# A two-layer graph network on one Trainium2 core: two destination blocks of attention 1 moved from dense steps to gathers

## The chip, the cores and the metric

The kernel runs on one core of a Trainium2 chip. The metric is device time in microseconds, the median of several executions. One further execution was recorded by the hardware profiler; all shares, durations and waits below come from that one.

## The reference

The input is a graph of 6250 nodes with 128 features and 200,000 edges, sorted by destination. Two residual blocks follow one another:

```python
h = relu(layernorm(x))
x = x + gat_2(elu(gat_1(h)))          # two attention layers
h = relu(layernorm(x))
x = x + conv(h, src, dst, edge_attr_4, edge_attr_8)

def gat_layer(x, W, attn_l, attn_r):   # H heads of D features
    feat = x @ W
    el, er = sum(feat * attn_l), sum(feat * attn_r)       # per node and head
    e = leaky_relu(el[src] + er[dst], 0.2)
    alpha = softmax of e over the edges of each dst
    return segment_sum(feat[src] * alpha, dst)
```

The first attention layer (attention 1) has four heads of 16 features, the second has one head. The convolution makes a message for each edge from the source's features and the edge's attributes and sums it by destination.

## The kernel before, in words

Nodes lie in NB = 49 blocks of P = 128. Attention 1 works on one destination block at a time, and in two different ways.

**Gathered blocks** are the first NG = NB - DENSE1 blocks, so 31. A window of 128 x 34 edges (K = 34) covers the edges of a block. `attending` takes them in five groups (`GROUPS`: four of 8 columns, one of 2). For each column `gather` (L319) has POOL issue one indirect DMA that fetches 128 rows of `table1` into the tile `G`, of which there are six buffers. `attend` then builds a one-hot of the destinations (`ohr`, L328, DVE), multiplies the transposed one-hot `oht` by the destination factors (L364, PE), forms weights and messages (L366 to L371, DVE), splits the messages into two halves (L335 on ACT, L336 on DVE) and sums them by destination on PE (L381). `load_low` fetches the 1088 KB from which `oht` is made, once for each block. After each fourth block, and after the last gathered one, `finish1` turns the sums into the tables of attention 2.

**Dense blocks** are the other DENSE1 = 18, taken in nine pairs by the generator `dense1`. They need no gathers: for every (source, destination) pair of nodes the number of edges is known, in `counts`. For each group of HS = 7 source blocks and each of the four heads, one step makes 7 ramps (L889, ACT), takes their minimum with the counts into `up` (L891, DVE), and later multiplies `up` by the source's features on PE (L909, 14 matmuls); once for each source group, PE also sums `every` (L903, 14 matmuls). A pair has a beginning (the tile `erb`), 4 x 7 such steps and an end. For each source group SP loads eight pieces of counts (`ctc`) and one of `rhs1` (`rc`, 717.5 KB), one group ahead.

**Counting** makes `counts` for all 49 blocks, in 196 steps of a quarter block: DVE makes one-hots `lo` and `key` (L771), PE multiplies them (L782), ACT copies the result (L784) and stores it. Attention 2 needs the counts of every block; the dense blocks of attention 1 need theirs before they are loaded.

The main loop runs over the gathered blocks and their groups, and hands out the other two kinds of step in proportion to the gathers done. Counting starts with block LAG = 3, dense steps with block LAG_D = 5:

```python
split = NG // (P // WB) * (P // WB)
order = [*range(split, NB), *range(split)]
n_dense = -(-DENSE1 // 2) * (2 + H1 * (NB // HS))
...
due = len(steps) * ((b - LAG) * K + s + n) // ((NG - LAG) * K)
...
due = n_dense * ((b - LAG_D) * K + s + n) // ((NG - LAG_D) * K)
```

`order` is the order of counting, beginning with the dense blocks. `n_dense` is 270. A step's later half (the scatter on PE, the matmuls of `up`) is issued one step later. The order written so is that of the program; the compiler's scheduling may shift single instructions on an engine's queue against it, and each queue then runs in its order.

Behind attention 1 all engines read a flag (L480) that decides whether blocks are done again. Then attention 2 runs, dense in all 49 blocks, and after it the convolution with 1563 gathers of its own.

Of the kernel before, what the change touches and what calls it, by code (L numbers as in the profile page):

```python
# [52 lines left out]
CT, LT = 30, 40  # L53
LAG = 3
AHEAD = 4
DENSE1, LAG_D = 18, 5
GP, GK, GSB = 125, 16, 4
SEG = 40
FAR = 1.0e30
# [1389 lines left out]
```

## Time and profile before

| what | us |
|---|---|
| median of 3 runs | 4578.62 (4572.18 to 4579.08) |
| profiled execution | 4562.61 |
| its span, first to last instruction | 4560.9 |
| first gather of attention 1 | at 110.4 |
| first gather of block 5 | at 389.3 |
| last gather of attention 1 begins | at 1751.7 |
| first work behind the flag at the end of attention 1 | at 1846.6 |

Times "at" are counted from the start of the span. In a line of a group, the columns are: line of the program, engine, operation, output and input tiles, shapes and count; then busy time and the mean of one in ns; then the idle time of the engine just before these instructions and what ended it. A line of a window holds its limits and length, busy time with the count of instructions for each engine, the granted TensorE clock as a share, the mean busy share of the DMA engines and the GB/s moved.

### The profile page before, as it was taken

The numbers are of one execution on the slowest core, as the hardware profiler recorded it, in microseconds if no ns is written. First come the engines' busy times: TensorE is split into PE (matmuls) and PEld (weight loads), VectorE is DVE, ScalarE is ACT, GpSimd is POOL, SyncE is SP. The second block draws the span as 40 slices with busy tenths as digits, with TensorE's granted clock in tenths as the row PEclk, the third lists the DMA queues.
The fourth block names the chain that finished last, engine by engine and source line by source line (L and its number), as shares of the span: only waits on it lengthen the run. The fifth ranks groups of instructions, "written<-read, shape, count | busy, mean of one in ns | idle before, by whom it ended". The sixth has DMA issues, their size and how long they took to land. (4 is left out here: it accounts for less than half of the span.)

```text
span 4560.9 us, 65476 instructions
## 1 busy us (share of the span) xinstructions
PE 3204.0 (70%) x21547; PEld 2371.8 (52%) x21548; DVE 3493.8 (77%) x5690; ACT 2829.5 (62%) x6841; POOL 2779.0 (61%) x2684
## 2 busy tenths in 40 slices
PE   4026576767776666499986777777777777777777
PEld 3015566656666666488884444444444444444444
DVE  5258687878887787588886788878778887877877
ACT  2025678788788788499985555555555555555554
POOL 0767777766766672100004777777777777777774
PEclk9998666666666676699997777677677767766776
DMA  4255555555555553544441222222222222222221
GB/s 109 67 140 147 149 155 159 157 155 158 167 161 149 150 166 120 209 156 152 170 156 44 59 59 59 58 56 59 58 59 58 58 57 57 59 58 58 58 58 32
DMA packets 348026, 480.87 MB, mean 105 GB/s; under 512 B 190601, under 2 KB 236207, under 8 KB 343694
## 3 DMA queue, kind: packets, MB, share of 16 engines
q1 hardware_dynamic: 199590, 240.46, 17.1%
q0 software_dynamic: 85776, 147.31, 12.9%
q10 hardware_dynamic: 62296, 88.68, 5.5%
q8 instruction: 176, 2.88, 0.3%
q14 instruction: 188, 1.54, 0.1%
HBM read 367.21 MB, written 108.97 MB: 104 GB/s over the span
## 5 line engine op out<-in xcount | busy, mean ns | idle before, releaser
L319 POOL DMA_INDIRECT G<-table,srcc x1563 | 1589.6, 1017 | 1028.4 <-DVE kept L1229 552.3
L319 POOL DMA_INDIRECT G<-table,srcw x1054 | 1118.0, 1061 | 510.5 <-issue 277.7
L1281 PE MATMUL whole<-halves,ohr 128*128 128x512 f32 x1563 | 681.2, 593 | 358.4 <-DVE halves L336 319.5
L889 ACT ACTIVATE ramp<-erb,sel 128x256 bf16<-128x256 f32 x1764 | 757.3, 499 | 15.5 <-DVE up L891 12.1
L1281 PEld LDWEIGHTS whole<-halves,ohr 128*128 128x128 f32 x1563 | 424.6, 286 | 602.0 <-DVE halves L336 390.5
L1262 ACT ACTIVATE g<-G,a 128x128 f32<-128x128 f32 x1563 | 510.2, 394 | 37.0 <-DMA G<-table,srcc 28.6
L1180 ACT ACTIVATE ramp<-small,sel 128x256 bf16<-128x256 f32 (+1 forms) x1225 | 447.8, 625 | 63.2 <-DVE up L1184 31.9
L784 ACT CAST ca<-small 128x392 bf16<-128x392 f32 x784 | 343.1, 482 | 189.5 <-PE small L782 179.2
L909 PE MATMUL up<-rc,up 128*128 128x102 bf16 x3528 | 311.2, 264 | 167.5 <-DVE up L891 166.2
L782 PE MATMUL small<-key,lo 128*128 128x98 bf16 x3136 | 316.1, 252 | 81.5 <-ACT ca L784 72.7
L909 PEld LDWEIGHTS <-up 128*128 128x128 bf16 x3528 | 266.5, 129 | 195.6 <-DVE up L891 189.4
L1251 PEld LDWEIGHTS big<-wtp_sb,hid 64*128 64x128 f32 x3126 | 259.1, 241 | 204.1 <-ACT hid L1245 100.0
L381 PE MATMUL whole<-halves,ohr 128*128 128x136 f32 x1054 | 231.9, 372 | 178.4 <-DVE halves L336 127.6
L336 DVE TENSOR_TENSOR halves<-big,halves 128x1024 fp32r<-128x1024 f32 x196 | 237.9, 1214 | 143.5 <-ACT halves L335 143.3
L1243 PE MATMUL small<-hid,wm_sb 128*128 128x512 f32 x392 | 289.4, 829 | 72.1 <-ACT hid L1241 72.1
L891 DVE TENSOR_TENSOR up<-ramp,ctc 128x1792 bf16<-128x1792 bf16 x252 | 273.9, 1088 | 85.7 <-ACT ramp L889 72.6
L1251 PE MATMUL big<-wtp_sb,hid 64*128 64x128 f32 x3126 | 310.0, 346 | 26.8 <-ACT hid L1245 26.8
L771 DVE TENSOR_TENSOR lo<-slots,turned 128x2048 bf16<-128x2048 bf16 x196 | 239.3, 1221 | 104.8 <-PE small L782 100.7
L1241 ACT ACTIVATE hid<-small 128x512 f32<-128x512 f32 x196 | 116.9, 596 | 312.8 <-PE small L1239 312.6
L782 PEld LDWEIGHTS <-lo 128*128 128x128 bf16 x3136 | 247.0, 124 | 112.9 <-issue 100.0
L335 ACT CAST halves<-mid 128x1024 fp32r<-128x1024 f32 x196 | 204.1, 1041 | 161.8 <-DVE mid L1270 160.1
L381 PEld LDWEIGHTS whole<-halves,ohr 128*128 128x128 f32 x1054 | 203.1, 278 | 190.2 <-DVE halves L336 135.6
(292 smaller groups left out, 6209.5 us busy)
## 6 DMA issues: line engine op xcount, KB each, us to landing
counts<-ca ACTq DMA_DIRECT2D x196, 392.0 KB
ct<-counts SPq DMA_DIRECT2D x196, 392.0 KB
rc<-rhs SPq DMA_DIRECT2D x63, 717.5 KB
oht<-dlow SPq DMA_DIRECT2D x31, 1088.0 KB
ctc<-counts SPq DMA_DIRECT2D x504, 56.0 KB
G<-table,srcc POOLq DMA_INDIRECT x1563
G<-table,srcw POOLq DMA_INDIRECT x1054
a8t<-attr_rows SPq DMA_DIRECT2D x391, 16.0 KB
```

What stands on the lines that cost most here:

```text
L319: nc.gpsimd.indirect_dma_start(out=G[:, c, :], out_offset=None, in_=table, in_offset=bass.IndirectOffsetOnAxis(ap=idx[:, c:c + 1], axis=0))
L381: nc.tensor.matmul(acc, oh[:, c, :], ms[:, c].rearrange("e s f -> e (s f)"), start=start and c == 0, stop=stop and c == n - 1)
L782: nc.tensor.matmul(ps[:, k * NKEY:(k + 1) * NKEY], lo[:, a, :, r], ky[:, a, :, r], start=True, stop=True)
L784: nc.scalar.copy(ca[:, :, i * W:(i + WBANK) * W].rearrange("p h (k d) -> p h k d", d=W), ps[:, :WBANK * NKEY].rearrange("p (k h d) -> p h ...
L889: nc.scalar.activation(ramp[:, i, :n * P], erb[:, h, :n * P], AF.Relu, bias=sel1[:, h0 + i, h:h + 1], scale=STEEP)
L891: nc.vector.tensor_tensor(up[:, :, :n * P].rearrange("p h (a d) -> p h a d", d=QN), ramp[:, :, :n * P].rearrange("p h (a d) -> p h a d", d ...
L909: nc.tensor.matmul(ups[k][:, h], up[:, i, k * P:(k + 1) * P], by_head[:, i, :, h, :], start=h0 + i + h == 0, stop=h0 + i + h == NB + H1 - 2)
L1180: nc.scalar.activation(ramp[:, h, :n * P], pe[:, :n * P], AF.Relu, bias=sel2[:, h0 + h, :], scale=STEEP)
L1243: nc.tensor.matmul(ph[:, :npr * P], wm2_sb, hid1[:, :npr * P], start=True, stop=True)
L1251: nc.tensor.matmul(pw[:, c, :], hid2[half, j * P:(j + 1) * P], wtp_sb[half].rearrange("x p u -> x (p u)"), start=True, stop=True)
L1262: nc.scalar.activation(g0[:, c], G[:, c, :], AF.Copy, scale=a0[:, c, :])
L1281: nc.tensor.matmul(acc, oh[:, c, :], ms[:, c].rearrange("e s h i u -> e (s h i u)"), start=start, stop=stop)
```

## The change

The number of dense blocks goes from 18 to 16.

```diff
-DENSE1, LAG_D = 18, 5
+DENSE1, LAG_D = 16, 5
```

All else follows from the constant. NG becomes 33, so blocks 31 and 32 are gathered, with 34 gathers and five groups each, and the pairs of dense blocks are eight, from (33, 34) to (47, 48). `n_dense` becomes 240, spread over blocks 5 to 32 instead of 5 to 30; the 196 counting steps are spread over blocks 3 to 32, and their order begins with block 32 instead of 30. The last group of `finish1` for gathered blocks has one block instead of three.

## The prediction

> **What bounds the kernel now.** I read the page's busy line and slices first, then the groups of lines for the shapes the edit touches, then the windows and the waits of attention 1 alone.
>
> ```profile
> PE 3204.0 (70%) x21547; PEld 2371.8 (52%) x21548; DVE 3493.8 (77%) x5690; ACT 2829.5 (62%) x6841; POOL 2779.0 (61%) x2684
> ...
> DVE  5258687878887787588886788878778887877877
> ACT  2025678788788788499985555555555555555554
> POOL 0767777766766672100004777777777777777774
> ```
>
> One slice is 114 us. POOL's row shows three stages: attention 1 with its gathers up to slice 16, attention 2 without POOL (zeros), and the convolution. Only attention 1 contains what is edited. In the timeline it ends at 1846.6 us, where all engines read a branch flag (L480); what follows is untouched, so the change is worth what it moves that instant.
>
> ```profile
> L319 POOL DMA_INDIRECT G<-table,srcw x1054 | 1118.0, 1061 | 510.5 <-issue 277.7 <-DVE w L366 74.3 <-DVE wseg_i L631 62.2
> L889 ACT ACTIVATE ramp<-erb,sel 128x256 bf16<-128x256 f32 x1764 | 757.3, 499 | 15.5 <-DVE up L891 12.1 <-DMA ctc<-counts 2.0 <-DMA counts<-ca 0.8
> L909 PE MATMUL up<-rc,up 128*128 128x102 bf16 x3528 | 311.2, 264 | 167.5 <-DVE up L891 166.2
> L891 DVE TENSOR_TENSOR up<-ramp,ctc 128x1792 bf16<-128x1792 bf16 x252 | 273.9, 1088 | 85.7 <-ACT ramp L889 72.6 <-DMA ctc<-counts 9.1 <-PE up L909 2.0
> L328 DVE TENSOR_TENSOR ohr<-slots,dstw 128x1024 fp32r<-128x1024 bf16 (+1 forms) x155 | 163.3, 1054 | 0.0
> ```
>
> A gather keeps POOL 1.061 us, and 0.30 us of issue precedes nearly each one, so a gathered block of K = 34 costs POOL some 46.3 us. The windows of the stage's steady part, and one block inside it:
>
> ```profile
> core 0: us, PE busy (x) PEld busy (x) DVE busy (x) ACT busy (x) POOL busy (x), PEclk, DMA share, GB/s
> 664.91:717.47 52.56, 36.41 (x368) 33.39 (x369) 40.94 (x65) 42.58 (x106) 40.27 (x39) 0.69 0.53 162
> ...
> 601.95:1846.57 1244.62, 846.21 (x8284) 771.74 (x8283) 987.78 (x1771) 1004.06 (x2490) 803.07 (x750) 0.66 0.52 153
> ```
>
> ACT is busy 1004.1 / 1244.6 = 81%, DVE 79%, PE 68%; POOL is 65% busy and, with its issue time, near 85%. No engine is full: ACT (ramp), DVE (up) and PE (up) hand each other work in order. Who leads is told by POOL's waits. In two groups of the page's fifth part, taken for 390 to 726 us and for 726 to 1696 us:
>
> ```profile
> L319 POOL DMA_INDIRECT G<-table,srcw x238 | 254.5, 1069 | 73.3 <-issue 65.8 <-DMA G<-table,srcw 4.6 <-DVE msg L371 1.0
> L319 POOL DMA_INDIRECT G<-table,srcw x613 | 656.0, 1070 | 284.8 <-issue 157.6 <-DVE w L366 74.0 <-DVE msg L371 16.6
> ```
>
> First POOL waits for nothing: blocks 5 to 11 start every (726.25 - 389.26) / 7 = **48.1 us**, its own pace with the run fetches between. From 726 us it waits until DVE frees a G buffer, and blocks start every (1695.07 - 726.25) / 18 = 53.8 us. So attention 1 is bound by the **ACT-DVE-PE chain**, with POOL 10% behind it as the next bound.
>
> **What the Trainium skill says.** "ScalarE: Activation LUTs", section "What ACT_TABLE_LOAD costs", gives an ACTIVATE with a pointer bias 280 ns + 0.833 ns per element, neighbours overlapping by 93 ns: 493 ns for 256 elements. The trace agrees: median 493 ns, 671.4 us busy for 1563 in the steady window, 0.43 us each. "GPSIMD Engine Reference", section "Key points", names POOL as the only engine for indirect gathers, so the added ones can go nowhere else; all 1054 are on POOL here. "Perfetto Trace Analysis", section "DMA Instruction — SWDGE (GPSIMD)", says the recorded interval is descriptor generation, not the move, so 1.061 us is queue time. "SBUF — State Buffer", section "SBUF: two separate sides", says some DVE modes lock POOL out of writing descriptors; gathers here range from 0.939 to 3.185 us beside a busy DVE, which fits but does not single that out.
>
> **The change part by part.** Two blocks leave the dense steps: 9 pairs become 8. The blocks with dense work become 28 (5 to 32) instead of 26, so a block carries 240/28 = 8.6 dense steps for 270/26 = 10.4, and 196/30 = 6.5 counting steps for 7.
>
> Removed, one pair, 28 steps (4 heads by 7 groups of seven source blocks):
> - ACT: 196 ramps x 0.43 = 84 us, with two erb copies and a copy of every, -86.
> - DVE: 28 x 1.088 = 30.5, and the end's reductions and products about 3.5: -34.
> - PE: 392 of 3528 up matmuls, 311.2/9 = 34.6; every (L903, 180.9 us in all) 20.1; erb and turns 4: -59.
> - SP: 7 loads of 8 ctc and one rc, near 4 us of issue each, -28 us, and 7 rc loads for which PE now and then waits (L903 waited 76.1 us in all, a ninth is 8.5).
>
> Added, two gathered blocks:
> - POOL: 68 x (1.061 + 0.30) = +93 us of queue.
> - DVE: the rows ohr, w, w, msg, msg, halves sum to 464.7 us over 155 groups, 3.0 each; ten groups 30, two oht 2.8, sums: +33.
> - ACT: ten halves at 0.577 and two sums: +6.
> - PE: (231.9 + 87.2) / 31 = 10.3 a block: +21.
> - SP: two oht loads of 1088 KB; the window loads and shifts were issued for the dense blocks too and only change place: nothing.
>
> finish1 runs as often (8 + 9 before, 9 + 8 after): nothing. Counting keeps all 196 steps: nothing. The first counted block moves from 30 to 32, so dense pair 33, 34 needs its 12 steps as early as pair 31, 32 did: about 13 of them are due when block 5 begins, so it is covered; uncovered it would cost one count, some 3 us.
>
> Net: DVE -1, ACT -80, PE -38, POOL +93. If DVE's work set the chain's time it would stay; if ACT's, it would fall by 80. The trace does not show which share applies, so I measure it on two neighbouring blocks. With the start of the first L368 of a block as its border, the window of L891 alone gives
>
> ```profile
> 877.80:910.71 32.91, 3.35 (x4) 0.70 0.49 127
> 910.71:989.93 79.22, 16.34 (x15) 0.67 0.52 158
> ```
>
> The first holds 3 steps (a record on its edge counts as a fourth) and 3 counts by the same windows of L771, the second 15 and 11. The 46.3 us between them are 12 steps and 8 counts; with a count at its DVE price (1.221 + 0.965 = 2.19) a dense step costs the chain (46.3 - 17.5) / 12 = **2.4 us**, between DVE's 1.09 and ACT's 3.0. A gathered block is then 32.9 - 3 x 2.4 - 3 x 2.19 = **19.1 us** of the chain. So: 2 x 19.1 - 28 x 2.4 = -29 us, -3.5 for the pair's end, and +7 for the start: in blocks 5 and 6 the DVE waits 35.5 us at L368 for gathers, and with 1.8 steps less per block 4.3 us of work less in each, the waits there grow by up to 8.7, of which I take most. Sum **-26 us**.
>
> POOL must allow it. From 389.3 us, 28 blocks at 48.1 are 1347, so its last gather could end at 1736; before, it ended at 1752.7 with about 110 us of waits for DVE in it and 94 us from there to the branch. At -26 the branch is at 1820.6, which leaves 85 us for waits and tail together. That fits: buffers six groups deep absorb the bunching, and the dense work queued behind the last gathers shrinks.
>
> The profiled execution took 4562.6 us (span 4560.9 and 1.7 around it), 16 under the median of 4578.6. So 4536.6 on its own scale, **4552.6** on the median's.
>
> **The rivals.** *DVE sets the chain.* DVE is 79% busy and its net is -1; waits "DVE up <- ACT ramp" total only 73 us in 252 steps. Then 0 to -5, less the start's 7: about 4578. Against it: ACT's 81% and the 2.4 us above.
>
> *POOL becomes the bound, slower.* Place: POOL's queue from block 5 on. It decides once the chain's block falls under 48.1 us: then the DVE, in order, stands at L368 with ups and counts queued behind it, as in blocks 5 and 6, ACT and PE stand behind the ups, and the pair's end and finish1 (about 10 us of DVE) no longer hide. 403.1 + 28 x 48.1 + 8 x 10 + 23 from the last sums to the branch = 1853, with some 15 of dense backlog 1868: +21, **4600**. For it: 48.1 is close to the 50 us that the chain would need. Against: after a pair's end POOL has gained a lead.
>
> *ACT sets the chain.* 28 x 3.0 - 6 is -78, but POOL's floor stops it: 1736 and a tail of 52, 1788, which is -59: 4520. *The constant does nothing* is excluded: it fixes both loops' counts.
>
> **How the numbers follow.** About 0.2%, 9 us, is what a measurement of this kernel can tell from no change. The chain at 2.4 us a step or at ACT's rate: 0.44; DVE's rate: 0.22; POOL's pace: 0.34, as 48.1 and the chain's 50 lie so close. Range 4520 to 4611: the ACT floor, and POOL's pace with gathers at 1.08 us instead of 1.069 (28 x 34 x 0.011 = 10 more; some blocks of the trace have such means). Cases of both signs share most of the chance; the forecast's own range is 4520 to 4569.
>
> **What would show it.** Right: gathers 1122, ramps 1568, up x224, oht x33; L480 near 1820 us; POOL's waits for L366 well under 74 us; blocks from 8 on starting 49 to 51 us apart; ACT's busy sum 80 us lower and DVE's equal. Wrong: L368 waiting over 80 us for G (POOL's pace), or blocks still 53 us apart (DVE's rate). A shift after L480 would contradict the whole reading.

## The result: 11 us faster, with the profile after

The kernel after takes 4562.62 us (median of 10 runs, 4544.91 to 4571.2), the kernel before 4573.78 (10 runs, 4563.37 to 4581.5). The ratio is 0.9981, interval 0.997 to 0.9993: a gain of 11 us, between 3 and 14, where 26 were forecast. The profiled execution took 4554.22, its span is 4552.3. Six runs of the study fell on two chips on which every kernel, the one before too, took some 23% longer (5635 us for 4574); they are compared only with their own runs of the kernel before.

Page of the kernel after, its first, second and fifth parts:

```profile
PE 3144.4 (69%) x21173; PEld 2330.2 (51%) x21174; DVE 3483.0 (77%) x5714; ACT 2761.1 (61%) x6654; POOL 2864.2 (63%) x2752
...
DVE  5257678688788787588885878778778887877877
ACT  2025677778778778599985545555455555555554
POOL 0767777777777773100004777777777777777774
...
L319 POOL DMA_INDIRECT G<-table,srcw x1122 | 1204.5, 1074 | 441.4 <-issue 304.8
L889 ACT ACTIVATE ramp<-erb,sel 128x256 bf16<-128x256 f32 x1568 | 671.1, 499 | 9.9 <-DVE up L891 7.7
L909 PE MATMUL up<-rc,up 128*128 128x102 bf16 x3136 | 282.3, 267 | 239.3 <-DVE up L891 235.3
```

And the row of L891 from the full list of that kernel's groups of lines:

```profile
L891 DVE TENSOR_TENSOR up<-ramp,ctc 128x1792 bf16<-128x1792 bf16 x224 | 243.2, 1087 | 52.3 <-ACT ramp L889 48.8 <-DMA ctc<-counts 1.9 <-issue 0.6
```

The counts are those of the edit (1122 gathers, 1568 ramps, 3136 matmuls of L909). PE's wait for `up` at L909 rose from 166.2 to 235.3 us, though there are 392 matmuls fewer: `up` comes later. POOL's row is 7 from slice 4 to slice 15, where 6 stood here and there; ACT's 7 and 8 of these slices are mostly 7 now. The rest of the span is untouched: the first work behind the flag comes at 1838.7 us, 7.9 earlier, and from there to the end are 2713.6 us where there were 2714.3. So in this pair of profiled executions the whole gain lies in attention 1, as read.

The windows from the span's start to that instant, before and after:

```profile
core 0: us, PE busy (x) PEld busy (x) DVE busy (x) ACT busy (x) POOL busy (x), PEclk, DMA share, GB/s
0.00:1846.57 1846.57, 1097.95 (x10449) 995.75 (x10451) 1343.94 (x2601) 1235.01 (x3012) 1176.06 (x1120) 0.74 0.50 143
...
0.00:1838.70 1838.70, 1057.64 (x10075) 964.07 (x10076) 1334.25 (x2625) 1162.82 (x2825) 1261.02 (x1188) 0.74 0.50 142
```

ACT lost 72 us of work, PE 40, DVE 10, and POOL gained 85. ACT is busy 63% of the stage and POOL 69%, and the stage is 8 us shorter: neither engine is full, and neither sum by itself tells how far the stage moves. POOL's own groups of lines, taken for 390 to 1770 us, first before, then after:

```profile
L319 POOL DMA_INDIRECT G<-table,srcw x884 | 945.2, 1069 | 379.9 <-issue 232.3 <-DVE w L366 74.3 <-DVE msg L371 29.7
...
L319 POOL DMA_INDIRECT G<-table,srcw x950 | 1032.1, 1086 | 310.2 <-issue 260.6 <-DVE w L366 14.8 <-DMA G<-table,srcw 14.3
```

Behind the second bar stands POOL's idle time, by what ended it. "Issue" is its own. Its waits for DVE to free a `G` buffer (L366, L371) were over 100 us and are some 20. The other side of that queue, the waits of L368 on DVE, in the view of that line's instructions, before and after:

```profile
  DMA G<-table,srcw: 61.3, 14
...
  DMA G<-table,srcw: 93.7, 16
```

DVE now waits longer for gathered rows. Behind 390 us these waits are 37 and 75 us (5.7 of the 75 are put down by the view to a run fetch, which stands in the same queue), before nearly all in blocks 5 and 6, after in blocks 5 to 9, 13 and 20. One such place, in DVE's timeline of the kernel after (start, length, instruction, and the idle time before it):

```profile
800.10 0.69 DVE L371 TENSOR_TENSOR msg<-G,msg 128x512 f32<-128x512 f32 x1
808.36 0.25 DVE L368 TENSOR_TENSOR w<-w,G 128x64 f32<-128x64 f32 x1 [7.57 <-DMA G<-table,srcw]
808.53 0.34 DVE L366 TENSOR_REDUCE w<-pe 128x64 f32<-128x192 f32 x1
808.80 0.42 DVE L827 TENSOR_TENSOR rr<-x,rr 128x260 bf16<-128x260 f32 x1
819.05 0.23 DVE L368 TENSOR_TENSOR w<-w,G 128x64 f32<-128x64 f32 x1 [9.84 <-DMA G<-table,srcw]
819.24 0.06 DVE L822 MEMSET rr<- 128x4 bf16 x1
819.39 1.09 DVE L891 TENSOR_TENSOR up<-ramp,ctc 128x1792 bf16<-128x1792 bf16 x1
```

Twice DVE stands at L368 for a group of eight gathers (POOL takes ten us for a group, at 1.25 each), and the `up` of L891 behind it comes only after. No wait stands before that `up`: its ramps were made.

### The profile page after: what moved, and what is told of

Its sections match the earlier page's. It is cut to its first block, busy times and chain, and to the rows that moved or that the text cites. A ratio compares the mean times of both kernels' runs of the same rounds, so it can differ in the third digit from the quotient of the medians.

```text
span 4552.3 us, 64537 instructions
## 1 busy us (share of the span) xinstructions
PE 3144.4 (69%) x21173; PEld 2330.2 (51%) x21174; DVE 3483.0 (77%) x5714; ACT 2761.1 (61%) x6654; POOL 2864.2 (63%) x2752
## 5 line engine op out<-in xcount | busy, mean ns | idle before, releaser
L319 POOL DMA_INDIRECT G<-table,srcw x1122 | 1204.5, 1074 | 441.4 <-issue 304.8
L889 ACT ACTIVATE ramp<-erb,sel 128x256 bf16<-128x256 f32 x1568 | 671.1, 499 | 9.9 <-DVE up L891 7.7
L909 PE MATMUL up<-rc,up 128*128 128x102 bf16 x3136 | 282.3, 267 | 239.3 <-DVE up L891 235.3
L381 PE MATMUL whole<-halves,ohr 128*128 128x136 f32 x1122 | 249.6, 362 | 187.0 <-DVE halves L336 136.5
L909 PEld LDWEIGHTS <-up 128*128 128x128 bf16 x3136 | 243.0, 131 | 263.5 <-DVE up L891 256.0
L1239 PE MATMUL small<-a8t,wm_sb 16*128 16x512 f32 x392 | 288.5, 823 | 10.5 <-DMA a8t<-attr_rows 10.5
L336 DVE TENSOR_TENSOR halves<-mid,halves 128x1024 fp32r<-128x1024 f32 x196 | 238.5, 1217 | 66.8 <-ACT halves L335 66.8
```

The source lines that it names most:

```text
L319: nc.gpsimd.indirect_dma_start(out=G[:, c, :], out_offset=None, in_=table, in_offset=bass.IndirectOffsetOnAxis(ap=idx[:, c:c + 1], axis=0))
L336: nc.vector.tensor_tensor(ms[1], m, ms[0], op=OP.subtract)
L381: nc.tensor.matmul(acc, oh[:, c, :], ms[:, c].rearrange("e s f -> e (s f)"), start=start and c == 0, stop=stop and c == n - 1)
L889: nc.scalar.activation(ramp[:, i, :n * P], erb[:, h, :n * P], AF.Relu, bias=sel1[:, h0 + i, h:h + 1], scale=STEEP)
L909: nc.tensor.matmul(ups[k][:, h], up[:, i, k * P:(k + 1) * P], by_head[:, i, :, h, :], start=h0 + i + h == 0, stop=h0 + i + h == NB + H1 - 2)
L1239: nc.tensor.matmul(ph[:, :npr * P], wm1_sb[:rows], a8t[:rows, :npr * P], start=True, stop=True)
```

## The experiments

Of the 26 us that were forecast, 15 are missing. Three explanations were put against each other. **The forecast's prices hold**, and POOL's queue, six `G` buffers deep, takes part of the gain back. **DVE leads**: then work taken from ACT is worth nothing, and the gain is chance. **The end of the stage**, the dense work behind the last gather, holds it. In the table, all in us, "block" is the mean distance of the first gathers of the blocks from 5 on, the last block counted to its last gather; "POOL waits" is POOL's idle time behind 390 us, beyond the 0.3 of issue before each instruction, "G waits" DVE's at L368 there; "tail" runs from the end of the last gather to the first work behind the flag ("end").

| kernel | gathered, dense | block | POOL waits | G waits | tail | end | ratio to before |
|---|---|---|---|---|---|---|---|
| before | 31, 18 | 52.4 | 119 | 37 | 94 | 1846.6 | 1 |
| after | 33, 16 | 49.0 | 21 | 75 | 79 | 1838.7 | 0.9981 (0.997 to 0.9993) |
| parts_less_b | 31, 16 | 51.4 | 89 | 46 | 96 | 1819.9 | 0.9932 (0.9916 to 0.9947) |
| parts_more_b | 33, 18 | 51.6 | 109 | 52 | 92 | 1923.8 | 1.0185 (1.0141 to 1.0229) |
| dense14_b | 35, 14 | 47.8 | 0 | 167 | 65 | 1882.6 | 1.005 (1.0033 to 1.0066) |
| early16 | 33, 16 | 51.4 | 98 | 48 | 17 | 1845.5 | 0.996 (0.9946 to 0.9974) |
| early18 | 31, 18 | 56.5 | 209 | 17 | 21 | 1875.2 | 1.0043 (1.0029 to 1.0057) |
| act_more16 | 33, 16 | 50.5 | 75 | 32 | 89 | 1888.6 | 1.0076 (1.0059 to 1.0093) |
| dve_more16 | 33, 16 | 49.5 | 22 | 64 | 82 | 1854.9 | 1.0016 (0.9999 to 1.0033) |
| pool_more16 | 33, 16 | 50.5 | 13 | 131 | 82 | 1909.5 | 1.0121 (1.0104 to 1.0138) |
| pool_more18 | 31, 18 | 53.5 | 94 | 57 | 96 | 1901.6 | 1.0084 (1.0067 to 1.01) |
| bufs8_18 | 31, 18 | 52.6 | 123 | 15 | 116 | 1859.2 | 1.0001 (0.9988 to 1.0013) |
| bufs8_16 | 33, 16 | 48.2 | 0 | 44 | 98 | 1821.8 | 0.9931 (0.9918 to 0.9944) |

"End" is one profiled execution. What lies behind it is the same work in all, and yet took between 2700.6 us (bufs8_18) and 2720.2 (bufs8_16), so an end is good to some 10 us, and the ratios decide.

**Each half of the change alone.** In the first, two blocks are neither gathered nor dense (blocks 31 and 32 get no sums of their own; `finish1` takes those of the last gathered blocks in their place); in the second, they are gathered and dense both, which makes 18 calls of `finish1` where before, after and the first half make 17.

```diff
-    NG = NB - DENSE1
+    NG, D0 = 31, NB - DENSE1          # parts_less, DENSE1 = 16
+    NG, D0 = 33, NB - DENSE1          # parts_more, DENSE1 = 18
...
-        for b0 in range(NG, NB, 2):
+        for b0 in range(D0, NB, 2):
```

> Only the dense part of the change: 16 dense and 31 gathered blocks; blocks 31 and 32 get no sums of their own, finish1 is given those of the last gathered blocks in their place. Theory A (POOL's pace joins in only when two gathered blocks are added): the chain loses 28 steps at 2.4 us and a pair's end, so the branch (L480) comes 71 us earlier than before, near 1776 us, the whole near 4502. Theory B (a dense step is worth less on the chain than 2.4 us, nearer to DVE's 1.09): 30 to 45 us earlier, near 4535.

> Only the gathered part: 18 dense and 33 gathered blocks; blocks 31 and 32 are worked out both ways. Theory A (the gathered block costs the chain 19.1 us, two parts don't add up because POOL sets the pace once both are in): branch 38 us later, near 1885, whole near 4612; with the other part alone at -71 the sum would be -33, not the -11 measured. Theory B (the parts add up; the prices were wrong): the two parts alone sum to about -11.

On the longer-running chip the ratios were 0.9942 (0.9921 to 0.9963) and 1.0253 (1.02 to 1.0306). Both ran once more on an ordinary one:

> Only the dense part once more: 16 dense, 31 gathered; blocks 31 and 32 get no sums of their own, finish1 is given those of the last gathered blocks. Theory A: POOL is free to run at 26 blocks x 48 to 49 us, so the chain's saving shows until that floor: branch between 1740 and 1776, 71 to 105 us earlier than before. Theory B (a dense step is worth less than 2.4 us on the chain): 30 to 45 us earlier.

> Only the gathered part once more: 18 dense, 33 gathered, blocks 31 and 32 worked out both ways. The dense part alone moved the branch by -27 us. Theory C (the parts add up, both prices of the forecast were too high, a gathered block costs near 9.5 us): branch 15 to 25 us later than before. Theory A (a gathered block costs the chain 19.1 us, and POOL's pace beside it): 38 us later or more.

Neither price was met, and the first half fell short of both ranges expected of it: removing a pair alone brought the end forward by 26.7 us (the forecast's steps make 71), adding two blocks alone pushed it back by 77 (38). Starting from the other kernel the same halves are worth 85 (parts_more_b to after) and 19 (parts_less_b to after). So the two prices don't add: what a half is worth depends on the other. The table shows where the misses sit: in the distance of the blocks, not in start or tail. A block carries 10.4 dense steps before, 9.6 in parts_more_b and 9.2 in parts_less_b, and the blocks shrink from 52.4 only to 51.6 and 51.4, with POOL waiting for the chain about 100 us in each. At 2.4 us a step and 2.2 a count they should have shrunk by 2.8 both times. The missing 1.8 over 26 blocks and 2.0 over 28 are 46 and 56 us; the halves missed by 44 and 39.

**Two blocks more, two fewer.** `DENSE1` at 14 and at 20.

> DENSE1 = 14: 35 gathered, 14 dense. Theory A (POOL's pace sets 16 already: 49.0 us a block from block 5 and a tail of 79): last gather at 387 + 30 x 49.0 = 1857, branch near 1930, whole near 4655 (+90 on 16). Theory B (the chain sets it, 16 lost only its start): a further -10 to -26 on 16, near 4540 to 4552.

> DENSE1 = 20: 29 gathered, 20 dense. Both theories have the chain as the bound here: 28 steps more at 2.4 us and a pair's end, two gathered blocks of 19.1 us less, +33 on the kernel before, near 4607. If the optimum is flat because prices are nearly equal (a dense step near 1.3 us), it is within 9 us of before.

> DENSE1 = 14 once more, 35 gathered, 14 dense; in the first try every kernel, the one before too, took 5600 us and more, with waits on PE's own queue that the trace of before does not have. Theory A (POOL's pace of 49.0 us a block sets 16 already): last gather at 387 + 30 x 49.0 = 1857 and the branch (L480) near 1930, 80 to 90 us later than before. Theory B (the chain sets 16, and it lost only at the start): 10 to 26 us earlier than with 16.

```diff
-DENSE1, LAG_D = 16, 5
+DENSE1, LAG_D = 14, 5
```

On the longer-running chip 14 gave 1.0113 (1.0056 to 1.0171) and 20 gave 0.9992 (0.9964 to 1.0021); 20 was run there alone. The three edits that ran on both kinds of chip (14 and the two halves) kept their sign. At 20 the 33 us that the forecast's prices make, 0.7%, did not come: another miss of these prices, as in the first half. On the ordinary chip 14 is 25 us slower than before. Its end comes 36 us later than before's and 44 later than after's, which neither theory had: with 49.0 us a block, taken for POOL's own pace, 80 to 90 were expected. Its POOL groups of lines for 390 to 1820 us, and its waits of L368:

```profile
L319 POOL DMA_INDIRECT G<-table,srcw x1016 | 1089.8, 1073 | 309.7 <-issue 279.3 <-DMA G<-table,srcw 16.2 <-DVE ohr L328 3.7
...
  DMA G<-table,srcw: 175.0, 39
```

No wait for a `G` buffer beyond the 0.3 of issue is left: POOL runs at its own pace, 47.75 us a block, and the view counts 39 waits of DVE for it. That is the rival "POOL becomes the bound" by itself. 16 lies between: 49.0, with 21 us of waits.

**The end of the stage.** Both hand-outs finish two blocks (68 gathers) early:

```diff
-            due = n_dense * ((b - LAG_D) * K + s + n) // ((NG - LAG_D) * K)
+            due = min(n_dense, n_dense * ((b - LAG_D) * K + s + n) // ((NG - LAG_D) * K - 68))
```

and the counting steps in the same way.

> 16 dense, and the dense and counting steps are handed out over 68 gathers (two blocks) fewer, so that none is left behind the last gathers. Theory A (POOL paces, and what stands behind its last gather is a tail of 79 us that overlaps with nothing): the chain fills its waits for gathers with that work, tail 35 to 50 us, branch 25 to 40 us earlier than with 16, near 1800 to 1815. Theory B (the chain's whole work sets the time): no change against 16, within 6 us.

> 18 dense as before, with the same earlier handing out. Theory A: here the chain is the bound and POOL has 100 us of waits; the tail shrinks, but the blocks get as much longer: within 8 us of before, save for the 36 us that the chain waits for gathers in blocks 5 and 6, of which up to 15 may be filled. Theory B: the same, no change.

The tail fell to 17 and 21 us, and the end didn't come earlier; at 16 it came 6.8 us later than after's, at 18 it came 28.6 later than before's, where 8 at most were expected. The work taken out of the tail lengthens the blocks, to 51.4 and 56.5 us, while POOL waits. So the tail, shortened in this way, gave nothing back. early16's ratio is better than after's, but the intervals still touch (0.997 to 0.9974), and its profiled execution, the fastest of five, shows no gain in attention 1: there it is the 2700.9 us behind the flag that are shorter, at a granted clock of 0.77 for 0.76. Whether early16 is better than after is not shown.

**One engine loaded more.** An unused operation for each dense step (ACT, DVE), two more gathers for each block (POOL), a repeated matmul at L364 (PE), at 16; POOL also at 18:

```diff
+                    nc.scalar.activation(spare[:, :n * P], erb[:, h, :n * P], AF.Relu, ...)   # act_more16
...
+                    nc.vector.tensor_tensor(spare, ramp[:, :3, :208], ramp[:, 3:6, :208], op=OP.min)   # dve_more16
...
+        if s in (8, 24):                                                  # pool_more16, pool_more18
+            spare = dn.tile([P, 1, R1], F32, name="spare")
+            gather(spare, table1, srcw[:, b, s:s + 1], 1)
...
-            nc.tensor.matmul(pe[:, c * 6 * H:(c + 1) * 6 * H], oht[:, c, :], pq, ...)
+            for _ in range(2):                                            # pe_more16
+                nc.tensor.matmul(pe[:, c * 6 * H:(c + 1) * 6 * H], oht[:, c, :], pq, ...)
```

> 16 dense, and each of the 224 dense steps makes one more ramp on ACT into a tile that nobody reads: 224 x 0.43 = 96 us of ACT. Theory A (DVE leads: the stage is DVE's work over a constant share of about 0.78, and ACT has slack): branch 0 to 20 us later than with 16 alone. Theory B (a dense step costs the chain 2.4 us, most of it ACT's ramps): 60 to 96 us later.

> 16 dense, and each dense step has one more tensor_tensor on DVE over 128x624 bf16 into a tile that nobody reads, near 0.42 us: 94 us of DVE. Theory A (DVE leads): 94 to 120 us later than with 16 alone. Theory B (chain priced at 2.4 a step, of which DVE is 1.09): about 40 us later.

> 16 dense, and two gathers more in each of the 33 blocks, into a tile that nobody reads: 66 x 1.385 = 91 us of POOL's queue. If POOL has nearly become the second bound at 16 (only 21 us of its waits are left behind block 5): 40 to 75 us later, with the added time as DVE's waits for G. If POOL is still covered: 0 to 15 us.

> 18 dense, as before, with the same two gathers more in each of the 31 blocks: 62 x 1.37 = 85 us of POOL's queue. POOL has 119 us of waits behind block 5 there: 0 to 20 us later, by the longer wait for gathers at the start.

> 16 dense, each of the 1122 small matmuls of L364 done twice with the same result: 1122 x 0.083 = 93 us of PE and as much of weight loads. If PE has slack beside ACT and POOL: 0 to 25 us later. If the order of the chain makes every engine count: 45 to 90 us.

What was added, as groups of lines of the first three:

```profile
L895 ACT ACTIVATE spare<-erb,sel 128x256 bf16<-128x256 f32 x224 | 110.6, 494 | 0.0
...
L895 DVE TENSOR_TENSOR spare<-ramp 128x624 bf16<-128x624 bf16 x224 | 106.5, 476 | 17.8 <-ACT ramp L889 17.3
...
L319 POOL DMA_INDIRECT spare<-table,srcw x66 | 66.8, 1012 | 37.4 <-issue 23.9 <-DMA spare<-table,srcw 13.2 <-DMA G<-table,srcw 0.3
```

The windows up to the end, for ACT, DVE and PE:

```profile
0.00:1888.60 1888.60, 1083.56 (x10075) 982.97 (x10076) 1342.05 (x2625) 1252.36 (x3049) 1246.67 (x1188) 0.72 0.49 138
...
0.00:1854.90 1854.90, 1060.71 (x10075) 967.55 (x10077) 1414.75 (x2849) 1163.95 (x2825) 1272.30 (x1188) 0.73 0.50 141
...
0.00:1854.33 1854.33, 1124.04 (x11197) 1033.67 (x11198) 1335.88 (x2625) 1162.90 (x2825) 1248.81 (x1188) 0.74 0.50 141
```

An engine's busy time rose by less than its own row has (89 for 110.6 on ACT, 80 for 106.5 on DVE), because neighbouring records overlap. Against the kernel after, the end moved by 50 us for ACT's 89 us of busy time more (0.56 for each us), by 16 for DVE's 80 (0.2), by 71 for POOL's 66.8 + 23.9 = 91 (0.78), and by 16 for PE's 66 (0.24; the ratio to before is 1.0003, 0.9992 to 1.0014). By the ratios the same four are 43, 16, 64 and 10 us, each good to some 10, so PE's is barely clear of noise. For ACT and DVE neither range expected was met (0 to 20 or 60 to 96; 94 to 120 or about 40). In these two edits hundreds of the instructions on DVE and PE also stand elsewhere in the order; what order alone can do is measured below. "DVE leads" falls all the same: with DVE leading, its own load would have counted nearly in full and ACT's hardly. Part of ACT's 50 may be PE's: its busy time up to the end rose from 1058 to 1084 us with the same matmuls, at a granted clock of 0.72 for 0.74.

POOL's load counts most, with the order of the instructions on PE and ACT the same as in the kernel after, and on DVE in all but 47 places. Part of it is the start: 20 of the 66 added gathers stand ahead of block 5 in POOL's queue, and block 5's first gather comes 26 us later. The other 46, with their issue 61.7 us, cost 45: 0.73. At 18 the same split is 25 us at the start, and 30 for the other 42 gathers' 56.5: 0.53, in a queue that waits 94 us for the chain. At most 20 us in all were expected at 18, and why it is more is not settled.

**Two more `G` buffers.** This leaves POOL's work as it is and changes how long it is stopped:

```diff
-    gath = one.enter_context(tc.tile_pool(name="gath", bufs=6))
+    gath = one.enter_context(tc.tile_pool(name="gath", bufs=8))
```

> 16 dense with eight G buffers for six; no other queue's order changes. POOL waits only 21 us there. If POOL's pace leads (pool_more16: 0.78 us of stage for each us of POOL), those 21 us come off, branch 10 to 20 us earlier. If the chain's own work is the floor as well (as early16 suggests), within 6 us.

> The kernel before with eight G buffers for six; no other queue's order changes. POOL's 119 us of waits behind block 5 fall, its last gather ends 40 to 80 us earlier. If the chain leads there, the branch stays within 8 us. If the chain pays for gathers that come late because POOL stood at a full set of buffers, it comes 10 to 25 us earlier.

At 18 nothing: 4569.93 us for 4570.91. At 16, 4540.70: 30 us faster than before, and with eight buffers the change of this study is worth 29 us instead of 11. The order of the instructions on PE, ACT and DVE is the same as with six; in POOL's queue 48 of some 1190 stand elsewhere, run fetches among the gathers, and at 18 about as many do (50). So neither the buffers nor that order give anything by themselves: the gain needs the 16. POOL's groups of lines of bufs8_16 for 390 to 1770 us, and its waits of L368:

```profile
L319 POOL DMA_INDIRECT G<-table,srcw x941 | 1021.1, 1085 | 286.9 <-issue 258.8 <-DMA G<-table,srcw 15.5 <-DVE msg L370 2.4
...
  DMA G<-table,srcw: 68.3, 11
```

The wait for L366 is gone from the row. The same row for 0 to 390 us, six buffers first, then eight:

```profile
L319 POOL DMA_INDIRECT G<-table,srcw x173 | 173.3, 1002 | 131.5 <-DVE wseg_i L631 62.2 <-issue 44.5 <-DVE msg L371 18.2
...
L319 POOL DMA_INDIRECT G<-table,srcw x182 | 184.1, 1011 | 121.3 <-DVE wseg_i L631 62.2 <-issue 49.1 <-DVE msg L371 4.6
```

Block 5's first gather comes at 374.4 us instead of 386.9, since ahead of it POOL waited for DVE to free a buffer (L371) for 4.6 us in place of 18.2; then 28 blocks at 48.2 instead of 49.0. POOL's last gather so ends 35 us earlier; the tail is 18 us longer, and the end comes 17 us earlier. This version beats both kernels.

**The order alone.** Any edit of the counts changes where the steps are handed out, and so the order on every queue. To see what order can do, both divisors were cut by 3 gathers (as in early16, with 3 for 68). This adds and removes no work; the steps are due 0.3% sooner:

> 18 dense; dense and counting steps are due as if the gathers were 3 fewer (0.3%), so the work and its pace are those of the kernel before, and only the order in which it stands on the queues differs. If order doesn't matter: branch within 4 us of 1846.6. If order alone moves the stage: 10 to 45 us either way, which is what the parts' misses need.

> 16 dense, the same shift of 3 gathers. If order doesn't matter: branch within 4 us of 1838.7. If it does: 10 to 30 us either way; as POOL's pace leads at 16, less than at 18.

Both fell on a longer-running chip. order18 against before there: 1.0071 (1.0047 to 1.0096); order16 1.013 (1.009 to 1.017), with no run of the kernel after beside it. So a shift that small, which is in effect the order alone, moves this kernel by 0.7% on such a chip, more than the change itself does on an ordinary one. How much on an ordinary chip is open, and with it how much of any line of the table that changes the counts is order; the comparison of six buffers with eight is free of this but for POOL's run fetches.

## Why the prediction was wrong in size, point by point

The step that failed is "POOL must allow it": the forecast found that POOL's queue has room on average and put what it and DVE cost each other by stopping in turn at nothing, but for +7 us at the start. If the rest of its sum, -32.5, is left standing, the measured -11 needs some +21 where +7 stood. Two more buffers show 18 us of that: with them the change is worth 29 us instead of 11.

- **Work moved: right, but for POOL's size.** ACT -72 up to the flag for -80, PE -40 for -38, DVE -10 for -1. POOL took 85 us of busy time and 27 of issue (277.7 to 304.8) for 93, 13 of it because the gathers of the whole stage became longer (1.074 us in the mean for 1.061). The gain is where it was placed, ahead of L480.
- **The chain's prices, 2.4 and 19.1 us: their net held, they didn't.** -29 - 3.5 made -32.5; with eight buffers, where POOL at 16 is stopped by DVE nowhere behind block 5, the medians give -29 and the ends -37. But each half alone missed by some 40 us: each step fewer shortens a block by 0.9 us between 10.4 and 9.2 steps (before to parts_less_b), and by 2.4, the forecast's price, between 9.6 and 8.6 (parts_more_b to after, 51.6 to 49.0 us). So the slope of two neighbouring blocks of one trace holds for one of these pairs of kernels and not for the other; that the errors cancelled was luck. The forecast's own stretch could have warned: from 726 to 1695 us a block holds 9.6 dense steps and 6.9 counts, which at its prices is 19.1 + 23.1 + 15.1 = 57 us, and the blocks start 53.8 apart. In the two blocks steps and counts rise together (3 and 3, then 15 and 11), so they don't tell one price from the other. Whether the order of the steps or a real threshold makes the plateau isn't shown.
- **"POOL must allow it": the step that failed.** The blocks did start 49.8 us apart from 8 on (their first L368, 546.85 to 1742.17), L891's wait for the ramps fell from 72.6 to 48.8, and POOL's waits for L366 fell from 74.3 to 14.8. But the sentence that "buffers six groups deep absorb the bunching" was argued and not measured. POOL's last gather ended at 1759.5 where 1736 could be: 21 us of waits, and 950 gathers of 1.086 us for 1.069, which is 16, less some 13 for an earlier start (2.4) and for what is left over of the queue. Then 79 us of tail: 103 us behind 1736 in place of 85, and 1838.7 in place of 1820.6. bufs8_16 takes away the stops, those ahead of block 5 too, and its end is 1821.8, with gathers as long (1.085).
- **The start's +7 was the mis-sized term.** It priced DVE's waits for gathers in blocks 5 and 6 alone. There they fell, from 35.4 to 18.1 us; but others came in blocks 7 to 9, 13 and 20, and in all they are 38 us more. With eight buffers 31 of them are gone again, and the medians say that this and POOL's stops together are worth 18.
- **The rival "POOL becomes the bound"** named the right place, and its mark came: L368 waited 93.7 us for `G`, over the 80 that were to show it. Its +21 us didn't come. It erred in taking the two paces as alternatives; within 2 us of each other they alternate: up to block 13 it is DVE that waits for POOL; behind it the blocks start 48.7 us apart, and now the one and now the other stops. Alone the rival holds at 14 (47.75 us a block, for 48.1).
- **DVE sets the chain**: excluded by dve_more16 (0.2 a us). **ACT sets the chain**: about half right by act_more16 (0.56, by the ratios 0.49); the bound that the rival saw in POOL stands in its way here too.

The gathers' mean, 1.086 us for 1.069, stays unexplained, but it isn't the missing gain: it is the same in bufs8_16. The Trainium skill, "SBUF — State Buffer", section "SBUF: two separate sides", says that some DVE modes lock POOL out of writing descriptors; DVE's busy share between block 5 and the last gather is 79% in both kernels, and bufs8_16 (1.085) and dense14_b (1.073) differ from each other as well, so no run singles that out.

## What to carry to other kernels

When work moves from one engine to another whose pace is within a few per cent, the forecast is not the smaller of two block times: here both queues stopped each other in turn, and the depth of the buffer between them decided how much of the gain was left. Try the change with a deeper buffer and without. A queue's pace is its busy time and its issue gaps and its stops; compare that with the pace the rest will have after the change, from the first block on and not only where the stage is steady. A price per step from two neighbouring blocks of one trace is a guess: check that the prices add up to the mean block, and run one half of the change alone.

## What the runs showed of the hardware

- A gather of 128 rows keeps POOL's queue 0.94 us at least and 0.30 us of issue, 1.25 in a quiet run of the timeline; the mean behind 390 us is 1.07 to 1.09.
- Near balance, work added on any of four engines made the stage longer. At 16, one us more on POOL (behind block 5), ACT, PE and DVE came with 0.73, 0.56, 0.24 and 0.2 us: the sum is over 1, with none busy above 79% between block 5 and the last gather. Each is good to some 0.1, and for ACT and DVE the order changed as well.
- With more ACT work the granted TensorE clock of the stage was 0.72 for 0.74, and the same matmuls took 26 us longer (act_more16). With more work on DVE it was 0.73, and the matmuls took 3 us longer. Which caused which isn't shown.
- The order in which the same work stands on the queues moved the whole kernel by 0.7% (order18, on a longer-running chip).
